# Attention with a mixture-of-experts layer on one core: loads of the opening on one queue, Wk split by two other engines, part of the next loads moved forward

## The chip, the cores and the metric

The kernel runs on one core of a Trainium2 chip. The metric is the device time in microseconds (us); less is better. The program is built with Bass and its Tile framework: inside a block called `manual_schedule` every engine runs its instructions in the order in which they are written, elsewhere a scheduler orders them, and semaphores are put in where one engine needs another's data. An engine works through its own list in order, so an instruction that waits holds up all that stand behind it.

## The reference, cut to what matters

```
# x: (2, 512, 512); 32 query heads, 8 key/value heads, head size 128
q, k, v = x @ Wq, x @ Wk, x @ Wv
probs = softmax(causal(q @ k.T / sqrt(128)))
x = layernorm(x + (probs @ v) @ Wo)
base = x @ W_base.T + b_base
w = sparsemax(x @ W_router.T + b_router)                 # 8 experts
expert = sum_e w[e] * (x @ lora_A[e]) @ lora_B[e]        # rank 16
out = layernorm(x + base + expert)
```

Everything is in 32-bit floating point. The kernel reaches that precision with several matmuls for each product: an operand is cut into a high and a low part, and high x high, high x low and low x high are added up.

## The kernel before

The work is cut into eight groups `g` (one key/value head with its four query heads), two batches `b` and four row tiles `i` of 128 queries. A unit (g, b, i) computes scores `s`, softmax weights `phl` (cut in two), their transpose `pt` (a DMA transpose issued by SP), the product `pv` with the values, and the output projection `pw`, which VectorE adds to the rows of x in the tiles `acc`. Beside the units of one group run the projections of the next: `pk`, `pq` and `pvp`, for K, Q and V.

The change lies in the first 60 us. For group 0 no scales are known yet, so the weights and x are cut in another form: `hi` is a rounded copy, `lo` is the difference (`WR` for weights, `XR` for x; the profile's tiles `wr` and `xr`). The opening is written out by hand, in one `manual_schedule` block:

- It starts with ten warm-up matmuls on zeros (`wps<-warm`, line 69).
- Loads: Wk of group 0 (tile `raw`, `load_w(4)`), the four 128-row chunks of batch 0's transposed x (`xraw`), then Wq0, Wq1, Wv, Wq2, Wq3, then batch 1's chunks of transposed x, four blocks of Wo, batch 0's transposed x again (`raw_x`), and batch 0's rows of x (`load_x(0)`, into `acc`). Chunks 0 and 2 of x are issued by ScalarE, all others by SP.
- The first projection, `PK[4]` (K of batch 0; 12 of the matmuls `park<-xr,wr`), goes chunk by chunk. For each of the four, ScalarE makes `hi` of x (`x_hi`, line 579), VectorE `lo` of x (`x_lo`, line 582), and GpSimd `hi` and `lo` of that chunk of Wk (lines 619 and 620). The other five projections follow, each of 12 matmuls, with ScalarE making `hi` and VectorE or GpSimd `lo` (lines 572 and 576).
- Maxima (`amax`, line 118, on VectorE; tile `mx`), squares (line 596) and a sum over the partitions (`total`, tile `tot`) then give the scales, by which K, Q and V leave PSUM as pairs of 16-bit tiles (lines 228 and 229).
- V is transposed by a DMA transpose (`vt`), and behind it SP issues the six blocks of W1, the weights of group 1 (tile `w1raw`), which lie in the space that `XR[0]` used (tags `base0` and `base1`).

After the block, in the scheduled part, `prepare(1, ...)` takes the maxima of the W1 blocks, finds their scales and cuts them. The rows of x of batch 1 are loaded at the first unit of batch 1 (`load_x(1)` at s == NT). These loads and `pt` are all issued by SP.

The tag `raw` has six buffers. A DMA into one waits until the last reader of what lay there is done. The tag `acc` has eight, which hold the transposed x (`xraw`) first and the rows of x later.

Of the kernel before, what the change touches and what calls it, by code (L numbers as in the profile page):

```python
# [8 lines left out]
F32 = mybir.dt.float32  # L9
# [5 lines left out]
ALU = mybir.AluOpType  # L15
AX = mybir.AxisListType

P = 128
NB, S, HID = 2, 512, 512
NT = S // P  # L20
KC = HID // P
# [15 lines left out]
def kernel(  # L37
# [18 lines left out]
    nc = tc.nc  # L56
    const = ctx.enter_context(tc.tile_pool(name="const", bufs=1))
    sb = ctx.enter_context(tc.tile_pool(name="sb", bufs=1))
# [6 lines left out]
    warm = const.tile([P, S], BF16, tag="warm", name="warm")  # L65
    nc.vector.memset(warm, 0.0)
    wps = ps.tile([P, S], F32, tag="PV", name="wps", bufs=1)
    for j in range(10):
        nc.tensor.matmul(wps, warm[:, :P], warm, start=True, stop=True)
    ident = const.tile([P, P], F32, tag="ident", name="ident")  # L70
    make_identity(nc, ident)
# [13 lines left out]
    def f(ap):  # L85
        return ap.bitcast(F32)
# [3 lines left out]
    def sync_load(dst, src):  # L90
        with tc.issue_after(hist[-3]) if len(hist) > 2 else nullcontext():
            return nc.sync.dma_start(dst, src)
# [4 lines left out]
    def load_raw(src, name, rows=False):  # L97

        raw = sb.tile([P, 512], F32, tag="rawo" if rows else "raw", name=f"raw_{name}", bufs=4 if rows else 6)
        sync_load(raw, src if len(src.shape) == 2 else src.rearrange("p a c -> p (a c)"))  # L100
        return raw
# [35 lines left out]
    def source(g, j):  # L137

        if j < 4:
            return wq[g * HPG + j]  # L140
        if j < 6:
            return (wk, wv)[j - 4][g]
        r0 = (g * HPG + j - 6) * P
        return wo[r0 : r0 + P, :]
# [43 lines left out]
    def halves(tags, name, shape):  # L188
        return [sb.tile(shape, F32R, tag=t, name=f"{name}{q}", bufs=n) for q, (t, n) in enumerate(tags)]
# [26 lines left out]
    def load_x(b):  # L216
        for t in range(b * NT, b * NT + NT):
            acc[t] = sb.tile([P, HID], F32, tag="acc", name=f"acc{t}", bufs=8)
            sync_load(acc[t], x_rows[t])

    def mm3(dst, pairs, first=True, last=True):
        n = len(pairs)
        for j, (a, b) in enumerate(pairs):
            nc.tensor.matmul(dst, a, b, start=first and j == 0, stop=last and j == n - 1)  # L224
# [9 lines left out]
    WR, XR = {}, {}  # L234

    def project(dst, g, b, j, chunks=range(KC)):
        pairs = []
        for c in chunks:
            if g:
                w2, x2 = W[(g, j)], xT[b]  # L240
                wh, wl, xh, xl = w2[:, 0, c, :], w2[:, 1, c, :], x2[:, 0, c, :], x2[:, 1, c, :]
            else:
                wh, wl, xh, xl = (a[:, c, :] for a in (*WR[j], *XR[b]))
            pairs += [(wh, xh), (wh, xl), (wl, xh)]
        mm3(dst, pairs, chunks[0] == 0, chunks[-1] == KC - 1)
# [18 lines left out]
    def pj(name, tag="pj"):  # L264
        return ps.tile([P, S], F32, tag=tag, name=name, bufs={"pj": 2, "S": 4}.get(tag, 1))
# [292 lines left out]
    JS = (4, 0, 1, 5, 2, 3)  # L558
    ROWS = (6, 7, 8, 9)
    mx = sb.tile([P, 24], F32, tag="mx0", name="mx0")  # L560
    x_raw = [[sb.tile([P, S], F32, tag="acc", name=f"xraw{b}_{c}", bufs=8) for c in range(KC)] for b in range(NB)]
    XR[0] = halves((("base0", 1), ("base1", 1)), "xr0", [P, KC, S])
    XR[1] = halves((("xr0", 1), ("xr1", 1)), "xr1", [P, KC, S])
    w_raw, PK = {}, {}
    ET = mybir.EngineType

    def load_w(j):
        w_raw[j] = load_raw(source(0, j), f"0_{j}")
        WR[j] = halves((("w", 12), ("w", 12)), f"wr{j}_", [P, KC, P])

    def w_hi(j, copy):
        copy(WR[j][0].rearrange("p a c -> p (a c)"), w_raw[j])

    def w_lo(j, engine):
        hi, lo = (a.rearrange("p a c -> p (a c)") for a in WR[j])
        engine.tensor_tensor(lo, w_raw[j], f(hi), ALU.subtract)

    def x_hi(b, c):
        nc.scalar.copy(XR[b][0][:, c, :], x_raw[b][c])

    def x_lo(b, c, engine):
        engine.tensor_tensor(XR[b][1][:, c, :], x_raw[b][c], f(XR[b][0][:, c, :]), ALU.subtract)
# [4 lines left out]
    def w_max(j):  # L587
        amax(mx[:, j : j + 1], w_raw[j])
# [7 lines left out]
        nc.scalar.activation(junk, raw, AF.Square, accum_out=dst)  # L596

    with tc.manual_schedule(engines={ET.PE, ET.DVE, ET.Activation, ET.Pool, ET.SP}):
        nc.scalar.dma_start(x_raw[0][0], xt[0, :, 0, :])
        load_w(4)  # L600
        nc.scalar.dma_start(x_raw[0][2], xt[0, :, 2, :])
        for c in (1, 3):
            nc.sync.dma_start(x_raw[0][c], xt[0, :, c, :])
        for j in JS[1:]:
            load_w(j)
        for c in range(KC):
            nc.sync.dma_start(x_raw[1][c], xt[1, :, c, :])
        wo_raw = [load_raw(source(0, j), f"0_{j}", True) for j in ROWS]
        x0_raw = [load_raw(xt[0, :, c, :], f"x0_{c}") for c in range(KC)]
        load_x(0)  # L610

        sq0 = sb.tile([P, 8], F32, tag="sq", name="sq0", bufs=2)
        sq1 = sb.tile([P, 8], F32, tag="sq", name="sq1", bufs=2)
        PK[4] = pj("park4", "pj")
        for c in range(KC):
            hi, lo = (a[:, c, :] for a in WR[4])
            raw = w_raw[4][:, c * P : (c + 1) * P]
            x_hi(0, c)
            nc.gpsimd.tensor_scalar(hi, raw, 1.0, 1.0, ALU.mult, ALU.mult)
            nc.gpsimd.tensor_tensor(lo, raw, f(hi), ALU.subtract)  # L620
            x_lo(0, c, nc.vector)
            project(PK[4], 0, 0, 4, [c])
        w_hi(0, nc.scalar.copy)
        w_lo(0, nc.vector)
        park(0, "pj")
        w_hi(1, nc.scalar.copy)
        w_lo(1, nc.gpsimd)
        park(1, "PV")
        w_hi(5, nc.scalar.copy)
        w_hi(2, nc.scalar.copy)  # L630
        w_lo(2, nc.gpsimd)
        w_hi(3, nc.scalar.copy)
        w_lo(3, nc.gpsimd)
        for c in range(KC):
            x_max(0, c)
        w_max(4)
        w_max(5)
        amax(mx[:, 6:7], mx[:, 9:13])
        for j in range(4):
            w_squares(sq0[:, j : j + 1], w_raw[j], "S")  # L640
        nc.scalar.activation(sq0[:, 4:7], mx[:, 4:7], AF.Square)
        w_lo(5, nc.vector)
        tot = total(sq0, 7, "0", "S")
        park(5, "wo")
        for c in (0, 1):
            x_hi(1, c)
            x_lo(1, c, nc.gpsimd)
        sc = sb.tile([P, 2, 8], F32, tag="sc0", name="sc0")
        SC[(0, False)] = sc
        scales(sc, tot, 7)  # L650
        x_factors(0, sc, 6)
        end_k(0, 0, PK[4])
        end_q(0, 0, 0, PK[0])
        factors(0, 0)
        end_q(0, 0, 1, PK[1])
        for c in (2, 3):
            x_hi(1, c)
            x_lo(1, c, nc.gpsimd)
        park(2, "S")
        for c in range(KC):  # L660
            x_max(1, c)
        amax(mx[:, 7:8], mx[:, 13:17])
        end_v(0, 0, PK[5])
        park(3, "S")
        for k in range(4):
            w_squares(mx[:, 17 + k : 18 + k], wo_raw[k], "S")
        amax(sq1[:, 1:2], mx[:, 17:21])
        nc.scalar.activation(sq1[:, 0:1], mx[:, 7:8], AF.Square)
        end_q(0, 0, 2, PK[2])
        tot = total(sq1, 2, "1")  # L670
        convert = split_x(0, x0_raw)
        next(convert)
        end_q(0, 0, 3, PK[3])
        sc1 = sb.tile([P, 2, 8], F32, tag="sc1", name="sc1")
        scales(sc1, tot, 2)
        SC[(0, True)] = sc1[:, :, 1:3]
        x_factors(1, sc1, 0)
        next(convert)

        w1 = [sb.tile([P, KC, S], F32, tag=f"base{q}", name=f"w1raw{q}") for q in range(2)]  # L680
        w1_raw = []
        for n, j in enumerate(JS):
            w1_raw.append(w1[n // 4][:, n % 4, :])
            sync_load(w1_raw[n].rearrange("p (c d) -> p c d", c=KC), source(1, j))

    def step_live():

# [90 lines left out]
    for s in range(len(units) - NT):  # L778
        if s < len(units):
            g, b, i = units[s]  # L780
            k = s // NT
            nx = groups[k + 1] if k + 1 < len(groups) else None
            if s == NT:
                load_x(1)
            done(unit_a(g, b, i))
            step_live()
            if nx:
                for j in ((4, 0), (1,), (5,), (2, 3))[i]:
                    proj(*nx, j)
                    advance()  # L790
            step_live()
        if s >= LB:
            done(unit_b(*units[s - LB]))
            step_live()
            advance()
        if s >= LC:
            n = s - LC
            u = units[n]
            done(unit_c(*u, n % NT == 0))
            step_live()  # L800
            if u[0] == NG - 1 and u[2] < NT - 1:
                live.append(ffn(u[2]))
        advance(True)
        if s == len(units) - 2 * NT:
            bias_row()
# [58 lines left out]
```

## Time and profile before

| | |
|---|---|
| median of 3 runs | 697.12 us (696.96 to 697.23) |
| the profiled execution | 697.11 us, of which 694.9 us are its span |
| TensorE matmul | busy 98% of the span |
| VectorE | 77% |
| ScalarE | 53% |
| GpSimd | 35% |
| DMA | 78.08 MB moved, 112 GB/s in the mean |

The span runs from the first instruction to the last. In the lines of the profile, PE is TensorE, DVE VectorE, ACT ScalarE, POOL GpSimd, SP the queue that issues most DMAs; L118 is line 118 of the kernel. A line of a timeline gives the start in us, the time it took, the engine, the line, the operation, the output and inputs with their shapes, and in brackets the idle time before it with what ended it. In the list of waits the three numbers are the total in us, how often, and the longest. Where one line joins several instructions, its time runs from the start of the first to the end of the last.

### The profile page before, as it was taken

The page shows a single profiled execution, that of the slowest core. Times are in us where ns is not written, and L with a number is a line of the kernel's source. Part 1 is how long each engine was busy: PE and PEld are TensorE (multiplying, and loading weights), DVE is VectorE, ACT ScalarE, POOL GpSimd, SP SyncE. Part 2 cuts the span into 40 slices and gives each one's busy share as a digit, 9 for nine tenths or more (in the row PEclk, how much of TensorE's full clock was granted, in tenths as well). Part 3 has the DMA queues.
Part 4 walks back from the last instruction along what each step waited for, and adds up shares of the span by engine and source line. Part 5 has one row for each costly group of instructions (what it writes and reads, how often), then busy time and mean ns, then how long its engine had stood idle before and what let it go on. Part 6 is the DMA issues. An engine that isn't in the chain of part 4 may idle for free.

```text
span 694.9 us, 10948 instructions
## 1 busy us (share of the span) xinstructions
PE 681.7 (98%) x3444; PEld 353.1 (51%) x3444; DVE 534.5 (77%) x1595; ACT 367.1 (53%) x1010; POOL 239.9 (35%) x334
## 2 busy tenths in 40 slices
PE   8999999999999999999999999999999999999996
PEld 5764545444544545454544545454544555554564
DVE  5798688778697778778697888778786785878786
ACT  5875754556365554656365554645465563446510
POOL 7665450624017150644116166146224000001022
PEclk9999999999999999999999999999999999999999
DMA  8649392637547293557448373916444261533511
GB/s 308 198 109 196 85 213 46 132 81 160 99 86 158 54 205 47 131 129 148 110 78 210 63 147 82 190 38 131 97 91 77 39 114 31 102 67 75 85 39 46
DMA packets 202026, 78.08 MB, mean 112 GB/s; under 512 B 186736, under 2 KB 186736, under 8 KB 201968
## 3 DMA queue, kind: packets, MB, share of 16 engines
q1 hardware_dynamic: 201680, 76.85, 51.1%
q8 instruction: 27, 0.44, 0.3%
q10 hardware_dynamic: 288, 0.52, 0.2%
q14 instruction: 31, 0.25, 0.1%
HBM read 29.12 MB, written 2.10 MB: 45 GB/s over the span
## 4 chain that ended last, share of the span: by engine, by line
PE 82%; DVE 8%; DMA 3%; ACT 3%; issue 2%; POOL 2%; POOLq 0%; DVEq 0%; ACTq 0%; SPq 0%
PE pw L224 20%; PE pq L224 19%; PE pv L224 13%; PE s L224 11%; PE pk L224 6%; PE pvp L224 5%; PE pa L224 4%; DVE phl L229 3%; PE park L224 2%; DVE s L342 1%; DMA raw<-in_wo_dram 1%; ACT s L347 1%; PE pb L224 1%; DMA pt<-phl 1%; ACT phl L228 1%
## 5 line engine op out<-in xcount | busy, mean ns | idle before, releaser
L347 ACT ACTIVATE s<-s,ast 128x128 f32<-128x128 f32 (+3 forms) x256 | 127.8, 499 | 165.5 <-DVE ast L342 163.7
L224 PE MATMUL pw<-w,o 128*128 128x512 f16 x768 | 176.9, 379 | 0.4 <-ACT o L228 0.2
L224 PEld LDWEIGHTS <-w 128*128 128x128 f16 x1008 | 97.8, 98 | 111.2 <-issue 0.8
L224 PE MATMUL pq<-xT,w 128*128 128x512 f16 x672 | 152.2, 379 | 0.0
L229 DVE SCALAR_TENSOR_TENSOR phl<-s,ast,phl 128x128 f16<-128x128 f32 (+3 forms) x256 | 124.6, 544 | 9.5 <-ACT phl L228 7.8
L228 ACT ACTIVATE phl<-s,ast 128x128 f16<-128x128 f32 (+3 forms) x256 | 116.7, 539 | 28.6 <-DVE ast L322 16.2
L342 DVE CUSTOM_DVE_ANT_0 s<-s,mask,lm 128x128 f32<-128x128 f32 (+3 forms) x256 | 126.6, 553 | 1.4 <-PE s L224 1.3
L224 PEld LDWEIGHTS <-o 128*128 128x128 f16 x768 | 74.7, 98 | 90.3 <-DVE o L229 0.8
L224 PE MATMUL s<-k,q 128*128 128x128 f16 (+3 forms) x768 | 117.7, 299 | 2.7 <-DVE phl L229 2.3
L224 PE MATMUL pv<-pt,vt 128*128 128x512 f16 x480 | 114.4, 379 | 1.6 <-DMA pt<-phl 1.6
L224 PEld LDWEIGHTS <-q 128*128 128x128 f16 x768 | 68.3, 98 | 50.6 <-issue 4.9
L256 POOL TENSOR_SCALAR lm<-sc,xs 128x1 f32<-128x1 f32 x15 | 4.0, 264 | 226.2 <-DVE sc L132 139.6
L115 POOL TENSOR_TENSOR w<-raw,w 128x512 f16<-128x512 f32 x68 | 77.2, 1155 | 0.3
L224 PEld LDWEIGHTS <-vt 128*128 128x128 f16 x480 | 46.7, 100 | 55.2 <-DMA pt<-phl 2.4
L396 DVE SCALAR_TENSOR_TENSOR acc<-pw,lm,acc 128x512 f32<-128x512 f32 x64 | 47.9, 748 | 33.0 <-PE pw L224 33.0
L229 DVE SCALAR_TENSOR_TENSOR o<-pv,o 128x512 f16<-128x512 f32 x64 | 43.9, 685 | 30.7 <-ACT o L228 30.5
L112 POOL TENSOR_SCALAR raw<-raw,sc 128x512 f32<-128x512 f32 x68 | 46.3, 692 | 57.6 <-DVE sc L133 57.6
L228 ACT ACTIVATE o<-pv 128x512 f16<-128x512 f32 x64 | 39.6, 618 | 34.3 <-PE pv L224 34.2
L118 DVE TENSOR_REDUCE mx<-raw 128x1 f32<-128x512 f32 x66 | 42.8, 678 | 14.7 <-DMA raw<-in_wo_dram 14.6
L347 ACT ACTIVATION_READ_ACCUMULATOR s<-s,ast 128x1 f32 x256 | 51.5, 201 | 0.0
L229 DVE SCALAR_TENSOR_TENSOR q<-pq,q 128x512 f16<-128x512 f32 x56 | 38.3, 688 | 15.1 <-ACT q L228 14.9
L228 ACT ACTIVATE q<-pq 128x512 f16<-128x512 f32 x56 | 34.0, 612 | 26.0 <-PE pq L224 25.8
(141 smaller groups left out, 612.1 us busy)
## 6 DMA issues: line engine op xcount, KB each, us to landing
raw<-in_wo_dram SPq DMA_DIRECT2D x32, 256.0 KB, 3.6
raw<-in_wq_dram SPq DMA_DIRECT2D x28, 256.0 KB, 4.5
raw_x<-in_xt_dram SPq DMA_DIRECT2D x8, 256.0 KB, 4.7
acc<-in_x_dram SPq DMA_DIRECT2D x8, 256.0 KB, 4.8
pt<-phl SPq DMA_TRANSPOSE x128, 3.8
out_dram<-y SPq DMA_DIRECT2D x8, 256.0 KB, 2.0
raw<-in_wk_dram SPq DMA_DIRECT2D x7, 256.0 KB, 3.6
raw<-in_wv_dram SPq DMA_DIRECT2D x7, 256.0 KB, 4.6
```

The costliest lines, as they stand in the source:

```text
L112: nc.gpsimd.tensor_scalar(view, view, by, 1.0, ALU.mult, ALU.mult)
L115: return first.ins, nc.gpsimd.tensor_tensor(lo, view, hi, ALU.subtract).ins
L118: nc.vector.tensor_reduce(dst, view, AX.X, ALU.max, apply_absolute_value=True)
L224: nc.tensor.matmul(dst, a, b, start=first and j == 0, stop=last and j == n - 1)
L228: nc.scalar.activation(hi, psrc, AF.Copy, scale=by)
L229: return nc.vector.scalar_tensor_tensor(lo, psrc, by, hi, ALU.mult, ALU.subtract).ins
L256: engine.tensor_scalar(lm[:, 4:5], sc[:, 0, 4:5], XS[b][0], 1.0, ALU.mult, ALU.mult)
L342: nc.vector.tensor_tensor_reduce(out=sc[:, :n], in0=sc[:, :n], in1=mask[:, S - n :], scale=lm[:, h : h + 1], scalar=BIG, op0=ALU.add, op1= ...
L347: nc.scalar.activation(sc[:, :n], sc[:, :n], AF.Exp, bias=st[:, 0, h : h + 1], scale=-1.0, accum_out=st[:, 1, h : h + 1])
L396: nc.vector.scalar_tensor_tensor(a, pw, LM[(g, b)][:, 7:8], a, ALU.mult, ALU.add)
```

## The change

The warm-up has nine matmuls. All first loads are issued by SP: x chunk 0, Wk, x chunks 1 to 3, then the weights as before. Wk is cut by ScalarE (`hi`) and VectorE (`lo`) in two pieces, chunk 0 and chunks 1 to 3, in place of GpSimd's eight instructions. W1's Wk and Wq0 are loaded into the tag `raw` behind `raw_x` and ahead of batch 0's rows of x; the other four blocks of W1 stay behind `vt`, all in the tag `base0`. Batch 1's rows of x are loaded directly behind those four, at the end of the block.

```diff
-    for j in range(10):
+    for j in range(9):
         nc.tensor.matmul(wps, warm[:, :P], warm, start=True, stop=True)
...
-        nc.scalar.dma_start(x_raw[0][0], xt[0, :, 0, :])
-        load_w(4)
-        nc.scalar.dma_start(x_raw[0][2], xt[0, :, 2, :])
-        for c in (1, 3):
+        for c in range(KC):
             nc.sync.dma_start(x_raw[0][c], xt[0, :, c, :])
+            if c == 0:
+                load_w(4)
...
         x0_raw = [load_raw(xt[0, :, c, :], f"x0_{c}") for c in range(KC)]
+        w1_raw = [load_raw(source(1, j), f"1_{j}") for j in JS[:2]]
         load_x(0)
...
         for c in range(KC):
-            hi, lo = (a[:, c, :] for a in WR[4])
-            raw = w_raw[4][:, c * P : (c + 1) * P]
             x_hi(0, c)
-            nc.gpsimd.tensor_scalar(hi, raw, 1.0, 1.0, ALU.mult, ALU.mult)
-            nc.gpsimd.tensor_tensor(lo, raw, f(hi), ALU.subtract)
             x_lo(0, c, nc.vector)
+            if c < 2:
+                n = slice(0, 1) if c == 0 else slice(1, KC)
+                hi, lo = (a[:, n, :].rearrange("p c d -> p (c d)") for a in WR[4])
+                raw = w_raw[4][:, n.start * P : n.stop * P]
+                nc.scalar.copy(hi, raw)
+                nc.vector.tensor_tensor(lo, raw, f(hi), ALU.subtract)
             project(PK[4], 0, 0, 4, [c])
...
-        w1 = [sb.tile([P, KC, S], F32, tag=f"base{q}", name=f"w1raw{q}") for q in range(2)]
-        w1_raw = []
-        for n, j in enumerate(JS):
-            w1_raw.append(w1[n // 4][:, n % 4, :])
-            sync_load(w1_raw[n].rearrange("p (c d) -> p c d", c=KC), source(1, j))
+        w1 = sb.tile([P, KC, S], F32, tag="base0", name="w1raw")
+        for n, j in enumerate(JS[2:]):
+            w1_raw.append(w1[:, n, :])
+            sync_load(w1[:, n, :].rearrange("p (c d) -> p c d", c=KC), source(1, j))
+        load_x(1)
...
-            if s == NT:
-                load_x(1)
             done(unit_a(g, b, i))
```

In the order that the scheduler gives, the maxima of W1's Wk and Wq0 now stand earlier in VectorE's list: the first ahead of the low part of V, the second between two score tiles of unit (0,0,0). On TensorE `pv` of unit (0,0,0) comes ahead of all `pvp` matmuls instead of behind six of them, and `s` of unit (0,0,3) follows `pw` of unit (0,0,0) with no `pq` matmuls between.

## The prediction

> **What bounds the kernel now.** I read the page first, then TensorE's waits, then the chain of waits for the first 60 us, then single engines' timelines where the chain changes hands.
>
> ```profile
> PE 681.7 (98%) x3444; PEld 353.1 (51%) x3444; DVE 534.5 (77%) x1595; ACT 367.1 (53%) x1010; POOL 239.9 (35%) x334
> ```
>
> TensorE is busy for 98% of the 694.9 us span, so a gap in it that closes early comes off the end: after the first 60 us its own waits add up to 2.0 us. Its waits of the first 75 us, in the list of waits (total, times, longest):
>
> ```profile
> PE pv L224 <- DMA pt<-phl: 1.3, 1, 1.3
> PE s L224 <- DVE phl L229: 1.2, 1, 1.2
> PE park L224 <- POOL wr L619: 0.4, 2, 0.2
> ```
>
> Three places. First the start, in the chain of waits (start us, us, what), where GpSimd's split of Wk paces the first projection:
>
> ```profile
> 0.72 4.23 DMA raw<-in_wk_dram
> ...
> 9.02 0.71 POOL wr L619
> ...
> 9.81 0.78 POOL wr L620
> ...
> 10.64 5.98 PE park L224 x25
> ```
>
> From 10.64 on TensorE has no gap for 20 us. Second, VectorE stands at the maximum of W1's Wk block, which has only then landed, with the softmax steps of unit (0,0,0) queued behind it (VectorE's timeline, then TensorE's):
>
> ```profile
> 29.95 0.69 DVE L118 TENSOR_REDUCE mx<-w1raw 128x1 f32<-128x512 f32 x1 [1.66 <-DMA w1raw<-in_wk_dram]
> ...
> 31.64 0.68 DVE L118 TENSOR_REDUCE mx<-w1raw 128x1 f32<-128x512 f32 x1
> 32.40 0.61 DVE L229 SCALAR_TENSOR_TENSOR phl<-s,ast,phl 128x128 f16<-128x128 f32 x2
> ```
> ```profile
> 32.81 0.82 PE L224 MATMUL s<-k,q 128*128 128x256 f16 x6 [1.16 <-DVE phl L229]
> 33.88 2.57 PE L224 MATMUL pq<-xr,wr 128*128 128x512 f32 x10 [0.25 <-DVE ast L322]
> ```
>
> Third, batch 1's rows of x stand in SP's queue ahead of the transposes of unit (0,0,2), and TensorE waits for those (SP's timeline; the chain; TensorE's timeline):
>
> ```profile
> 47.27 1.50 SPq L92 DMA_DIRECT2D acc<-in_x_dram  x3
> 48.95 4.44 SPq L95 DMA_TRANSPOSE pt<-phl  x2
> ```
> ```profile
> 50.66 5.86 DMA pt<-phl
> ```
> ```profile
> 56.56 2.12 PE L224 MATMUL pv<-pt,vt 128*128 128x512 f16 x9 [1.35 <-DMA pt<-phl]
> ```
>
> The change touches all three.
>
> **Part 1: the start.** Eight GpSimd instructions go (L619 x4 at 0.63, L620 x4 at 0.66 us mean: 5.1 us of the queue that paces the chain). ScalarE gains two copies of Wk, VectorE two subtractions, each 128x128 and 128x384. No row shows them in fp32r; nearest are 128x128 and 128x384 `phl`, 0.38 and 0.59 us on ScalarE, 0.35 and 0.61 on VectorE. Bounds: nothing, if all fits into waits (VectorE waits 5.4 us in all for `xr` here), and 0.9 us on each engine. I count them whole, as both engines now carry the chain.
>
> Loads: SP issues all five first ones at about 0.42 us each, so by 2.9; a load passes in 0.65 us (the semaphore events put Wq0, Wq1, Wv and Wq2 at 8.86, 9.51, 10.20 and 10.85). Now Wk lands at 4.95, x chunk 0 at 5.12, chunks 1 to 3 at 6.10, 6.60, 8.21. On one queue Wk still has one load ahead: 5.0. Chunk 0, first, lies between 3.6 and 5.1; I take 4.3. Chunks 1, 2: 5.65, 6.3; chunk 3 between 7.0 and 8.2.
> - ScalarE: x0 hi 4.3 to 4.95, Wk hi chunk 0 to 5.4, x1 hi 5.67 to 6.3, rest of Wk hi to 6.85, x2 hi to 7.5, x3 hi to 8.4 at worst.
> - VectorE (0.70 for an x lo): x0 lo to 5.7, Wk lo chunk 0 to 6.0, x1 lo 6.3 to 7.0, rest of Wk lo to 7.6, x2 lo to 8.3, x3 lo 8.4 to 9.1.
> - TensorE: chunk 0 from 5.4 at 0.43 us each, chunk 1's last at 7.6, chunk 2's three by 8.8, chunk 3's last issued about 9.4.
>
> Now it is issued at 10.64: 1.2 us. Wq0, landing at up to 8.86, has its low part by about 10.2 and takes some of that: I carry **1.1 us**, between 0.3 (all first data 0.8 later) and 1.6. Of ScalarE's sums of squares and VectorE's maxima, which end at 14.56 and 13.9 now, nothing moves later than TensorE needs for `tot` (15.3): slack 0.6 us. If it went, `tot` would wait for that much. GpSimd, freed, has Wq1's low part at 11.4; it is read at 12.9.
>
> The tenth warm-up matmul (0.43 us, ending 5.4) goes; it would have stood in the way of a start at 5.4. That costs nothing unless the clock suffers. The rows: warm-ups 0.43 us apart, parks from 11.2 on 0.23 apart; the fast spacing is there from about 7 us. [...] By the row, TensorE stood still for 0.5 us at 5.4 and was granted the clock all the same; here the gap is 5.0 to 5.4, and the first term stays 1.1. [...]
>
> **Part 2: two blocks of W1 sooner.** Their loads go ahead of batch 0's four rows of x: these land 1.3 us later (2 x 0.65), at under 24 us, and are first read at 49.8: free. W1's Wk and Wq0 land near 21, before VectorE reads them. But both maxima (0.6 us of VectorE's time each) now stand earlier. The first is ahead of V's low part, which releases the transpose `vt` and behind it W1's other four loads. So `vt` is issued at 24.67 - 1.1 + 0.6 = 24.17. It lands 4.2 us after issue, and the first and second loads behind it are there 1.0 and 2.45 us later (28.91, 29.93, 31.37 now): 29.4 and 30.9. VectorE reaches the third maximum at 29.0 and waits 0.4, ends it at 30.0, and waits for the fourth to 30.9. It does `phl` from 31.5 (32.40 now), K's low part to 32.75 (33.82). **The wait is not removed, it passes to the next two blocks**: TensorE, ready at 30.4, waits to 31.8 for `s` and to 32.8 for `pq`, against 33.88. The lead stays 1.1 us and doesn't grow: 0 from this part. Bound above: without the wait VectorE itself sets 32.1, 0.7 us more. Below: a landing 1 us later takes 1 us.
>
> **Part 3: batch 1's rows sooner.** SP issues four loads more ahead of `pt` of unit (0,0,0). [...] W1's loads now end at 34.17 and `pt`, issued at 33.04, lands at 35.45. With two loads more in all and the lead, the ring is empty near 34.9 and both `pt` have landed at 36.6. TensorE (now 38.8, with six `pvp` ahead that come after it in the new order, 1.4 us) is there at 36.2: a new wait of 0.4. By the row alone (2.5 us from issue at 33.9 to landing), 36.4 and 0.2. I take 0.4. By unit (0,0,1) VectorE and DMA have lead again, and about 0.3 comes back at the S buffers, which are free when TensorE comes to them. So the lead is 1.0 near 47 us. There `s` of unit (0,0,3) follows `pw` with no `pq` between, so its cover of 1.6 us is gone: `phl` is written at 46.0 and 46.5, TensorE needs it at 46.1 and 46.75: just in time.
>
> In return SP issues the transposes of unit (0,0,2) when `phl` is written, about 46.5 and 49.0, with no load in front: landed near 53, and TensorE comes at 55.2 - 1.0 = 54.2. The 1.35 us go whole. What is late next is the softmax of the same unit, within 0.5 us.
>
> **Sum**, against the profiled execution's own 697.11 us (span 694.9; median 697.12): 1.1 + 0 - 0.4 + 0.3 + 1.35 = 2.35, so 694.8. What follows runs with no gap, so nothing gives it back.
>
> **The rivals.**
> - Partly taken back (25%): first data later, a missed clock window, lost cover before `s` of (0,0,3), or pt later by a microsecond. Each takes 0.3 to 1; for it, VectorE and SP are tighter than before; against, none was a bound but by these loads. About 1.2 in all: 696.0.
> - W1's blocks are in time (20%). The window of DMA from 25 to 29 us shows one instruction fetch (q8) and a hole in `vt`'s transfer from 26.8 to 28. Without the collision, `vt` lands 1.5 us sooner and VectorE sets the pace: 0.7 + 0.3 more, 693.8. Against: fetch and `vt` both hang on VectorE's chain and move together.
> - Slower (6%): `pt` of unit (0,0,0) is stuck behind batch 1's rows. The transposes of unit (0,0,2) took 6.2 us from issue to landing behind three such loads. If `pt` takes that from 33.9, it lands at 40.1, 3.5 us after my 36.6, and the gain of 2.35 turns into a loss of 1.1; another collision of 1.5 makes it 699.6 at worst, 698.6 in the middle. It decides from a landing at about 39.
> - The change does nothing (4%): the waits move elsewhere in full, 697.1.
>
> **How the numbers follow.** Likeliest (45%): 694.8, by itself 694.0 to 695.6. 0.2% is 1.4 us, about what a measurement of this kernel can tell from no change; faster than that means under 695.7. All of the likeliest and of the second rival lie there, and a fifth of the first: 0.45 + 0.20 + 0.05 = 0.70. Same: the rest of the first, and the last: 0.24. Slower: 0.06. The range, 693.0 to 696.7, leaves out the slow case, the last, and the ends of the others.
>
> **What would show it.** Right: the last matmul of the first 12 parks starts between 9.2 and 10.3; `mx<-w1raw` still waits for its load near 29 to 31, under 1.7 us; `pv` at 54 does not wait for `pt`; `pv` near 36 does, by under 1 us. Wrong: the first 12 end later than 10.6 or run 0.43 us apart beyond 7 us; `pv` near 36 waits over 2 us; or a lead of 2 us at 60 us that is not there at the end.

## The result and the profile after

| | before | after |
|---|---|---|
| median | 697.72 us (696.96 to 698.78, 6 runs) | 694.33 us (693.16 to 695.05, 6 runs) |
| the profiled execution | 697.11 us, span 694.9 | 694.67 us, span 692.9 |

The ratio of the times is 0.9949, with a 95% interval of 0.9935 to 0.9962: 3.6 us less, between 2.7 and 4.5. The two profiled executions are 2.44 us apart, 2.06 of it inside the span (VectorE's last `y` starts at 689.14 us, 691.20 before); the other 0.4 lies outside it and has no row. The executions of one and the same kernel differ by the clock that TensorE was granted: of 129 of the kernel before, taken beside the experiments, 65 had a mean clock of 0.997 or more, as the two profiled ones have, and a median of 696.9 us, the others 698.6 us.

The page's first line is hardly changed, but for GpSimd's eight instructions that are gone:

```profile
PE 681.1 (98%) x3443; PEld 353.5 (51%) x3443; DVE 534.0 (77%) x1597; ACT 367.9 (53%) x1012; POOL 235.0 (34%) x326
```

TensorE's waits of the first 75 us (total, times, longest):

```profile
...
PE s L224 <- DVE phl L229: 0.8, 1, 0.8
PE park L224 <- ACT wr L622: 0.7, 2, 0.5
PE tot L123 <- ACT q L228: 0.3, 1, 0.3
PE pq L224 <- DVE k L229: 0.2, 1, 0.2
```

The wait of `pv` for `pt`, 1.3 us before, is not in the list any more. That of `s` for `phl` is smaller but still there. The start waits for ScalarE's part of Wk where it waited for GpSimd's. TensorE's timeline has the numbers (start, us, what; in brackets the idle time ahead and what ended it):

```profile
7.35 8.26 PE L224 MATMUL park<-xr,wr 128*128 128x512 f32 x33 [0.48 <-ACT wr L622]
15.45 0.28 PE L123 MATMUL tot<-sq,ones 128*128 128x7 f32 x2
...
31.96 0.81 PE L224 MATMUL s<-k,q 128*128 128x256 f16 x6 [0.83 <-DVE phl L229]
32.94 1.20 PE L224 MATMUL pq<-xr,wr 128*128 128x512 f32 x4 [0.17 <-DVE k L229]
...
36.63 0.81 PE L224 MATMUL pv<-pt,vt 128*128 128x512 f16 x3
...
54.22 2.12 PE L224 MATMUL pv<-pt,vt 128*128 128x512 f16 x9
```

Set against the kernel before, `tot` stood at 16.46 us there and stands at 15.45: a lead of 1.01. `s` came from 32.81 to 31.96 (0.85), `pq` from 33.88 to 32.94 (0.94), and `pv` of unit (0,0,2) from 56.56 to 54.22 (2.34). At the end of the span 2.06 are left.

VectorE's timeline shows why TensorE gained nothing more near 31 us. It now waits for the third block of W1 (Wq) where it waited for the first (Wk):

```profile
30.01 0.69 DVE L118 TENSOR_REDUCE mx<-w1raw 128x1 f32<-128x512 f32 x1 [0.75 <-DMA w1raw<-in_wq_dram]
...
31.56 0.61 DVE L229 SCALAR_TENSOR_TENSOR phl<-s,ast,phl 128x128 f16<-128x128 f32 x2
```

And SP's timeline has batch 1's rows (`acc`) directly behind W1's blocks and out of the way of the later transposes:

```profile
28.72 1.80 SPq L92 DMA_DIRECT2D acc<-in_x_dram  x4
...
46.34 12.74 SPq L95 DMA_TRANSPOSE pt<-phl  x4
```

### The profile page after: what moved, and what is told of

The parts are those of the page before. It is cut to its first block, busy times and chain, and to the rows that moved or that the text cites. A ratio compares the mean times of both kernels' runs of the same rounds, so it can differ in the third digit from the quotient of the medians.

```text
span 692.9 us, 10942 instructions
## 1 busy us (share of the span) xinstructions
PE 681.1 (98%) x3443; PEld 353.5 (51%) x3443; DVE 534.0 (77%) x1597; ACT 367.9 (53%) x1012; POOL 235.0 (34%) x326
## 4 chain that ended last, share of the span: by engine, by line
PE 82%; DVE 9%; ACT 3%; DMA 2%; issue 2%; POOL 1%; SPq 0%; POOLq 0%; DVEq 0%; ACTq 0%
PE pw L224 21%; PE pq L224 20%; PE pv L224 13%; PE s L224 12%; PE pk L224 5%; PE pvp L224 5%; PE pa L224 4%; DVE phl L229 3%; DVE s L342 1%; DMA raw<-in_wo_dram 1%; PE park L224 1%; ACT s L347 1%; DVE mx L118 1%; PE pb L224 1%; ACT phl L228 1%
## 5 line engine op out<-in xcount | busy, mean ns | idle before, releaser
L115 POOL TENSOR_TENSOR w<-raw,w 128x512 f16<-128x512 f32 x70 | 79.6, 1156 | 0.3
L118 DVE TENSOR_REDUCE mx<-raw 128x1 f32<-128x512 f32 x68 | 44.3, 678 | 15.8 <-DMA raw<-in_wo_dram 15.7
L228 ACT ACTIVATE q<-pq 128x512 f16<-128x512 f32 x56 | 34.0, 613 | 24.5 <-PE pq L224 24.3
```

The costliest lines, as they stand in the source:

```text
L115: return first.ins, nc.gpsimd.tensor_tensor(lo, view, hi, ALU.subtract).ins
L118: nc.vector.tensor_reduce(dst, view, AX.X, ALU.max, apply_absolute_value=True)
L228: nc.scalar.activation(hi, psrc, AF.Copy, scale=by)
```

## The experiments

The difference in us is worked out from the ratio and the median of the kernel before in the same group of runs (697.72 us for the change; 698.06 for runs 1 to 4, 697.5 for 5 to 8, 697.43 for 9 to 11, 698.02 for 12); the last column is the interval of the ratio in us.

| kernel | median us | ratio | difference us | interval |
|---|---|---|---|---|
| the change | 694.33 | 0.9949 | -3.6 | -4.5 to -2.7 |
| 1 start alone | 695.04 | 0.9958 | -2.9 | -4.0 to -2.0 |
| 2 two W1 blocks alone | 700.96 | 1.0039 | +2.7 | +1.7 to +3.6 |
| 3 batch 1's rows alone | 696.32 | 0.9978 | -1.5 | -2.2 to -0.8 |
| 4 change, four W1 blocks early | 693.27 | 0.9935 | -4.5 | -5.7 to -3.4 |
| 5 change without the rows | 696.4 | 0.9981 | -1.3 | -2.1 to -0.6 |
| 6 change without W1's blocks | 695.2 | 0.9961 | -2.7 | -3.7 to -1.7 |
| 7 change without the start | 701.56 | 1.0045 | +3.1 | +2.0 to +4.3 |
| 8 change, six W1 blocks early | 695.09 | 0.9952 | -3.3 | -4.7 to -2.0 |
| 9 before, stall filled | 698.04 | 1.0008 | +0.6 | -0.3 to +1.3 |
| 10 change, ten warm-ups | 694.51 | 0.9957 | -3.0 | -3.8 to -2.2 |
| 11 loads of the start alone | 696.53 | 0.9990 | -0.7 | -1.3 to -0.1 |
| 12 split of Wk alone | 697.1 | 0.9989 | -0.8 | -1.7 to +0.2 |

**1. The start alone**: nine warm-ups, first loads on SP, Wk split by ScalarE and VectorE.

```diff
-    for j in range(10):
+    for j in range(9):
...
+        for c in range(KC):
+            nc.sync.dma_start(x_raw[0][c], xt[0, :, c, :])
+            if c == 0:
+                load_w(4)
...
+                nc.scalar.copy(hi, raw)
+                nc.vector.tensor_tensor(lo, raw, f(hi), ALU.subtract)
```

> The kernel before with the new start alone (nine warm-ups, first loads on SP, Wk split by ScalarE and VectorE). My theory: the start is worth 1.1 us, everything in VectorE's chain up to the transpose vt moves with it, and with vt the loads of W1 behind it; so VectorE's wait for W1's Wk stays about 1.7 us long and is only passed earlier, and the wait of pv of unit (0,0,2) for pt stays at 1.3. Time 1.1 us under before. Rival: W1's landing is set by the DMA queue and not by vt, so the lead is eaten in that wait (it grows to 2.7 us) and the time is that of before.

It took 695.04 us. TensorE's waits of the first 75 us:

```profile
PE s L224 <- DVE phl L229: 1.7, 1, 1.7
...
PE pv L224 <- DMA pt<-phl: 0.7, 1, 0.7
```

In this execution TensorE's timeline lists no idle time between 5.3 and 15 us, and `tot` came at 14.94, 1.5 us sooner than before. But 0.5 us more of waiting for `phl` (1.7 against 1.2) took that much back: W1's loads stand behind `vt` in SP's list (issued from 26.12 and at 24.67 us in the kernel before), and the first of them was there only 0.87 us sooner (VectorE's maximum of it starts at 29.08 us, 29.95 before). One thing was not expected: `pv` of unit (0,0,2) waited only 0.65 us for `pt`, against 1.35, though batch 1's rows stood in SP's queue where they had stood before. In time the start is the largest part.

**2. W1's two blocks alone.**

```diff
+        w1_raw = [load_raw(source(1, j), f"1_{j}") for j in JS[:2]]
         load_x(0)
...
+        for n, j in enumerate(JS[2:]):
```

> The kernel before with two blocks of W1 loaded ahead of batch 0's rows of x alone. My theory: VectorE still waits, for the third block, by 0.4 to 1.1 us, and has spent 0.6 us more ahead of vt; the time is within 0.4 us of before. Rival, which is what the edit looks like: the wait of 1.66 us and TensorE's 1.16 us behind it go, and the time is 1.2 to 1.4 us under before.

It is slower than before, which neither theory had. VectorE's timeline tells why: with the old start the scheduler put the maximum of W1's Wk into VectorE's list directly behind `tot`, ahead of the scales, on which everything that cuts K and Q of batch 0 waits:

```profile
20.57 0.69 DVE L118 TENSOR_REDUCE mx<-raw 128x1 f32<-128x512 f32 x1 [3.57 <-DMA raw<-in_wk_dram]
21.18 0.16 DVE L132 TENSOR_SCALAR sc<-tot 128x7 f32<-128x7 f32 x1
```

VectorE stood for 3.57 us, and TensorE for 2.67 us ahead of its first `s`, at 27.75 us. (The list names ScalarE's squares, line 596, as what ended this wait; they stand behind K and Q in ScalarE's list, which start at 22.41 and 23.00 us, when the scales are there, and run from 25.75 us on.) So this run measures the place of the maxima, not the loads.

**3. Batch 1's rows alone.**

```diff
+        load_x(1)
...
-            if s == NT:
-                load_x(1)
```

> The kernel before with batch 1's rows of x loaded at the end of the opening block alone. My theory: pv of unit (0,0,2) no longer waits 1.35 us for pt, pt of unit (0,0,0) lands later but TensorE comes to it at 38.8 us only and doesn't wait; time 1.35 us under before. Rival: pt of unit (0,0,0) stands behind ten loads, TensorE waits 1 us or more near 39 us, and the time is that of before.

1.5 us less, which fits the 1.35 us of `pv`'s wait. Its trace shows less: `pv` of unit (0,0,2) still waited 0.43 us for `pt`, so that 0.9 of the 1.35 us were gone, and its profiled execution waited longer for `phl` than any other (2.0 us). TensorE's timeline:

```profile
57.72 2.12 PE L224 MATMUL pv<-pt,vt 128*128 128x512 f16 x9 [0.43 <-DMA pt<-phl]
```

**4. Four of W1's blocks early**, two more than in the change, in the space of `y`.

```diff
         w1_raw = [load_raw(source(1, j), f"1_{j}") for j in JS[:2]]
+        for j in JS[2:4]:
+            w1_raw.append(sb.tile([P, HID], F32, tag="y", name=f"w1y{j}", bufs=2))
+            sync_load(w1_raw[-1].rearrange("p (c d) -> p c d", c=KC), source(1, j))
```

> The changed kernel with four blocks of W1 loaded ahead of batch 0's rows of x instead of two (W1's Wq1 and Wv into the two buffers of tag y, which nothing else uses before the end). The scheduler reorders some instructions near 30 us. Theory that VectorE's wait for w1raw at 30 us (0.75 us in the changed kernel) costs TensorE time: it goes, and the time is 0.7 us under the changed kernel, the lead at 33 us is 1.6 to 1.8 us against 0.94. Rival: VectorE's own work sets the pace there, the lead stays under 1.2 us and the time is that of the changed kernel within 0.3 us.

693.27 us, the lowest of all. TensorE's waits of the first 75 us show the wait of `s` for `phl` gone, and what is late next, K's low part:

```profile
PE pq L224 <- DVE k L229: 0.6, 1, 0.6
PE pv L224 <- DMA pt<-phl: 0.3, 1, 0.3
```

The span is 690.7 us, 2.1 under the change's. `pk` began at 24.07 us, 0.8 sooner than in the change, and this lies ahead of the waits that the two blocks were to shorten; the waits near 31 us were shorter by 0.4, and `pv` of unit (0,0,1) gave 0.3 back. At `pv` of unit (0,0,2) it was 0.8 us ahead (53.42 against 54.22). The rest came later: `pk` of the next group began 1.55 us sooner (136.69 against 138.24). So most of the 2.1 us in this pair of traces is not the two blocks' wait. The interval overlaps the change's: that four blocks are better than two is likely, not certain.

**5. The change without batch 1's rows** (`load_x(1)` back at `s == NT`).

```diff
-        load_x(1)
...
+            if s == NT:
+                load_x(1)
```

> The changed kernel with batch 1's rows of x loaded at the first unit of batch 1 again (start and W1's two blocks kept). Theory: the transposes of unit (0,0,2) stand behind these loads again and TensorE waits 1 to 1.4 us for pt near 55 us; its time is about 1.4 us over the changed kernel's, 695.7 us, with a lead over the kernel before near 1.0 us up to 54 us and none gained there. Rival, that batch 1's rows were behind idle queues anyway and the gain came with the start: 694.3 us, no wait for pt near 55 us.

2.2 us slower than the change by the two ratios (0.0032). TensorE's timeline has the wait again, and SP's the rows between the transposes:

```profile
54.60 2.12 PE L224 MATMUL pv<-pt,vt 128*128 128x512 f16 x9 [0.82 <-DMA pt<-phl]
```
```profile
45.80 1.72 SPq L95 DMA_TRANSPOSE pt<-phl  x1
47.57 1.42 SPq L92 DMA_DIRECT2D acc<-in_x_dram  x2
49.08 9.46 SPq L95 DMA_TRANSPOSE pt<-phl  x3
```

In the traces the two are closer: `pv` waits 0.82 us more here, and the profiled executions are 0.55 us apart. Together with run 3, where the rows alone took 1.5 us off, this shows that the rows' place in SP's queue costs time. It does not show that all of the 1.35 us is the rows' (runs 1, 3 and 6).

**6. The change without W1's two blocks** (all six behind `vt`).

```diff
-        w1_raw = [load_raw(source(1, j), f"1_{j}") for j in JS[:2]]
...
+        for n, j in enumerate(JS):
```

> The changed kernel with all six blocks of W1 loaded behind vt again (start and batch 1's rows kept). Theory of the prediction, that the two blocks only pass VectorE's wait on to the next two: the same as the changed kernel, 694.3 us within 0.4. Rival, that they do shorten the wait: with the earlier start alone TensorE waited 1.7 us for phl near 30 us, so s of unit (0,0,0) waits 1.5 to 2 us here instead of 0.8 and the time is 695.1 to 695.6 us, and some runs have a lower mean clock than the changed kernel's.

0.8 us slower than the change by the ratios, with intervals that overlap. In the profiled execution `s` waited 1.20 us for `phl` against 0.83. And `pv` of unit (0,0,2) waited for `pt`, although batch 1's rows are out of the way here (TensorE's timeline, then SP's):

```profile
55.34 2.12 PE L224 MATMUL pv<-pt,vt 128*128 128x512 f16 x9 [0.49 <-DMA pt<-phl]
```
```profile
48.56 12.24 SPq L95 DMA_TRANSPOSE pt<-phl  x4
```

SP issued that transpose at 48.56 us, against 46.34 in the change. Without the two blocks VectorE's list has the old order, in which all four `phl` of this unit come together from 47.35 us on; in the change two come at 45.12 us and two at 47.49. So the blocks bring an order with them, and the last 0.5 us of `pv`'s wait goes with it: with rows and blocks both moved (the change, runs 4, 7, 8 and 10) no trace has that wait, with the rows moved and the old order both have (0.43 in run 3). All in all they are worth between nothing and some 2 us in time, and 0.4 and 0.5 us at these two waits in the trace.

**7. The change without the start.** The edit is run 1's, backwards.

```diff
-    for j in range(9):
+    for j in range(10):
...
+            nc.gpsimd.tensor_scalar(hi, raw, 1.0, 1.0, ALU.mult, ALU.mult)
+            nc.gpsimd.tensor_tensor(lo, raw, f(hi), ALU.subtract)
```

> The changed kernel with the old start (ten warm-ups, loads on two queues, GpSimd's split of Wk); W1's two blocks and batch 1's rows kept. Here the list order puts the maximum of W1's Wk directly behind VectorE's part of the scales, as in the kernel with the two blocks alone. Theory that the parts add up: 1.1 us over the changed kernel, 695.4 us. Rival, that the maximum's place in VectorE's list decides: VectorE stands 3 to 4 us at it near 20 us, TensorE waits over 2 us near 27 us and goes to half clock, and the time is 697.5 to 700 us.

The rival held in its mechanism, and the time, 701.56 us, lies above even its range. VectorE's timeline has the same place for the maximum as in run 2:

```profile
20.61 0.69 DVE L118 TENSOR_REDUCE mx<-raw 128x1 f32<-128x512 f32 x1 [3.47 <-DMA raw<-in_wk_dram]
```

The parts of this change don't add up, since one of them moves instructions that another one's loads feed. In the changed kernel the maxima stand behind those of batch 1's x, at 23.05 and 25.62 us, and don't wait.

**8. All six of W1's blocks early.**

```diff
+        for j, tag, w in zip(JS[4:], ("xf", "ffnbias"), (HID, HID + NE)):
+            w1_raw.append(sb.tile([P, w], F32, tag=tag, name=f"w1t{j}")[:, :HID])
```

> The changed kernel with all six blocks of W1 loaded ahead of batch 0's rows of x, none behind vt. Theory: with four blocks early (693.27 us) TensorE's wait for phl near 31 us is gone already, and what is left there is a wait of 0.6 us for K's low part; six take at most that: 692.7 to 693.3 us. Rival, that six loads more push batch 0's rows or the maxima into the way of vt: 693.8 us or more, with a wait for acc or phl on TensorE before 60 us.

The waits near 31 us are gone altogether in the trace (span 691.7 us), but `tot` waited 0.7 us at 24.5 us for ScalarE, and the time is 695.09 us, with a wide interval. That is the time of the rival, without the wait that it named. Four of its seven executions had a mean clock under 0.997. No run shows more to be had from W1's loads than four blocks give.

**9. Before, with the stall at 31.6 us filled.**

```diff
+            if s == 1:
+                fill = ps.tile([P, S], F32, tag="PV", name="fill", bufs=1)
+                with tc.issue_after(last_q):
+                    for j in range(6):
+                        nc.tensor.matmul(fill, warm[:, :P], warm, start=True, stop=True)
             done(unit_a(g, b, i))
```

> The kernel before with six matmuls on zeros (1.3 us of TensorE) put between the twelve pq and the s that waits for phl near 31.6 us; they compute nothing that is used. Nothing else is moved. Theory: TensorE's clock falls to half for a window of 3.4 us after a stretch in which it stood for more than about half of a window (it did in the traces with 2.0, 2.6 and 2.7 us of wait, not in those with up to 1.7 us), and executions with a mean clock under 0.997 are in good part such ones. Then filling the stall costs 0.1 to 0.3 us in the others, and the share of executions under 0.997 falls from a half to under a quarter: median 696.9 to 697.3 us against 697.5 to 698 of before. Rival, that the low clock has nothing to do with that stall (it is set at the start, or is there throughout): the share stays at a half and the median is 0 to 0.3 us above before's.

The theory fell: 7 of 14 executions still had a mean clock under 0.997, and the time is 0.6 us above before's, with an interval that includes no change at all. The edit was not clean, though. The scheduler moved two maxima ahead of the second pair of `phl`, and TensorE still waited for `phl` in two pieces, 0.58 us at 33.3 and 0.86 us at 35.96 us. The trace of this run has its half-clock window elsewhere, at the other end of the kernel. TensorE's timeline, then busy time and granted clock by stretch (the column behind POOL is the clock):

```profile
645.47 1.01 PE L224 MATMUL s<-k,q 128*128 128x256 f16 x6 [1.10 <-DVE phl L229]
```
```profile
core 0: us, PE busy (x) PEld busy (x) DVE busy (x) ACT busy (x) POOL busy (x), PEclk, DMA share, GB/s
644.40:647.90 3.50, 2.40 (x12) 1.47 (x12) 3.11 (x10) 2.19 (x7) 0.00 (x0) 0.99 0.83 155
647.90:651.30 3.40, 3.40 (x10) 2.66 (x9) 2.24 (x9) 2.30 (x10) 0.00 (x0) 0.50 0.41 79
```

A wait of 1.10 us like this one is in the traces of before (ahead of 643.84 us) and of the change (ahead of 642.07) too, and cost no window there: the granted clock is 1.00 from 642 to 660 us in both. In this trace a window followed, and so it did in run 10's (0.51 from 645.3 to 648.8 us) and run 7's (0.50 from 649.67 to 653.08 us).

**10. The change with ten warm-ups.**

```diff
-    for j in range(9):
+    for j in range(10):
```

> The changed kernel with ten warm-up matmuls again. By the row (the tenth is in the way of a start at 5.4 us and the clock needs it not): 0 to 0.3 us over the changed kernel, 694.3 to 694.6 us. [...]

694.51 us, the same as the change within its interval; in the trace the first `park` starts at 5.46 us instead of 5.41. The tenth is neither needed nor in the way. As a near twin of the change it also shows how much luck a profiled execution has: here `pv` at 37.29 us waited 0.69 us for `pt`, which in the change's own trace had landed 0.13 us before TensorE came.

**11. The loads of the start alone.**

```diff
-        nc.scalar.dma_start(x_raw[0][0], xt[0, :, 0, :])
-        load_w(4)
-        nc.scalar.dma_start(x_raw[0][2], xt[0, :, 2, :])
-        for c in (1, 3):
+        for c in range(KC):
             nc.sync.dma_start(x_raw[0][c], xt[0, :, c, :])
+            if c == 0:
+                load_w(4)
```

> The kernel before with only the loads of the start put on one queue (x chunk 0, Wk, x chunks 1 to 3); ten warm-ups and GpSimd's split of Wk kept. Theory: GpSimd's eight instructions pace the first projection from Wk's landing at 5.0 us, which doesn't move: nothing gained, as before within 0.3 us, the last matmul of the first twelve issued at 10.5 to 10.7 us. Rival, that the landing of x chunk 3 at 8.2 us paces it: up to 0.7 us faster.

0.7 us less, yet not at the start: GpSimd's last step (line 620 before, 619 here) is at 10.11 us, 9.81 before, and `tot` stands at 16.47 us against 16.46. GpSimd's timeline:

```profile
10.11 0.46 POOL L619 TENSOR_TENSOR wr<-raw,wr 128x128 fp32r<-128x128 f32 x1
```

The theory held for the start; where the 0.7 us come from is open; 16 of 22 executions had a mean clock of 0.997 or more, against half of before's.

**12. The split of Wk alone.**

```diff
-            nc.gpsimd.tensor_scalar(hi, raw, 1.0, 1.0, ALU.mult, ALU.mult)
-            nc.gpsimd.tensor_tensor(lo, raw, f(hi), ALU.subtract)
...
+                nc.scalar.copy(hi, raw)
+                nc.vector.tensor_tensor(lo, raw, f(hi), ALU.subtract)
```

> The kernel before with only the split of Wk given to ScalarE (high part) and VectorE (low part); loads on two queues and ten warm-ups as before. Theory: the gain at the start is the split's, up to what x chunk 3's landing at 8.2 us leaves: its high part at 8.9, low part at 9.6, the last matmul of the first twelve issued at 9.7 against 10.6 us, 0.8 us of lead; with the old place of the loads behind vt a gain of 0.7 to 1.5 us, 696.0 to 696.8 us. Rival, that loads and split help only together (chunk 3 late, Wk's pieces in front of x chunks 1 and 2): the last of the twelve at 10.3 us or later and the time within 0.4 us of before's.

0.8 us less, with an interval that includes no change at all. Its trace cannot decide, because in it TensorE stayed at the slow spacing to 10.5 us. Busy time and number of matmuls from 7.0 to 10.5 us, here and then in run 1:

```profile
7.00:10.50 3.50, 3.50 (x8) 2.28 (x8) 3.15 (x6) 3.42 (x7) 0.57 (x1) 1.00 1.04 399
```
```profile
7.00:10.50 3.50, 3.50 (x14) 2.23 (x14) 3.15 (x6) 2.72 (x6) 0.72 (x1) 1.00 1.01 387
```

Both are busy throughout, with 8 matmuls in one (0.44 us each) and 14 in the other (0.25 us each). `tot` came at 16.69 us, nothing gained. The clock column shows 1.00 in both; but in the trace's own clock record the full clock begins at 10.59 us here and at 6.93 us in run 1, and nothing is recorded ahead of that, so this slow start is to be read from the spacing. Ahead of it TensorE had stood from 5.62 to 6.11 us. Loads and split each give 0.7 to 0.8 us alone and 2.9 us together. In run 11 the chain was left on GpSimd, which was not moved; that here it was left on the landing of x is argued, not shown. The intervals are wide enough that the two could also just add up.

## Why the prediction was right, point by point

The sum was 2.35 us. The two profiled executions are 2.44 apart, the medians 3.4, and the interval begins at 2.7: the gain in time is larger than the sum by 0.3 us at least. Two things that the sum left out account for much of it.

The first is the clock. Of the kernels with the new start (the change, runs 1, 4 to 6, 8 and 10) 20 of 73 executions had a mean clock under 0.997, of the kernel before 64 of 129; at 1.7 us each, the estimate of the last section, that is some 0.4 us on average. The share differs from kernel to kernel (none of 6 in run 1, 4 of 7 in run 8), so this is rough, and why the new start should make such executions rarer is open. The second lies outside the span: 2.06 to 2.20 us in every one of the 129 executions before, 1.75 to 1.81 in all six of the change. That is 0.35 us which no step had, and why is open too.

Without both, the sum comes out well: over executions with a mean clock of 0.997 or more the median span is 694.8 us before (65 executions) and 692.3 for the change (5), 2.5 us less. The same comparison gives 1.65 for the start alone (run 1), 1.3 for the rows alone (run 3), 1.05 without the rows (run 5) and 2.1 without W1's blocks (run 6).

- **Start, 1.1 us.** Measured 1.01 at `tot` in the change's trace, which is the least of all with the new start: `tot` came between 14.94 and 15.45 us in the seven of them; with the old start it came between 15.96 and 16.65 (before and runs 2, 3, 7 and 9). The instructions cost what was counted: on ScalarE 0.30 and 0.51 us, on VectorE 0.28 and 0.55. One landing was off: x chunk 1 came at 6.24 us, not 5.65, and the last of the first twelve matmuls was issued at 9.77, not 9.4 (10.64 before). In time the start alone took 2.9 us off, more than its trace accounts for: there `s` is only 1.0 us ahead of before's (31.82 against 32.81), and the last `y` 1.2 (689.98 against 691.20). All six of its executions had a mean clock of 0.997 or more, which is one part of the difference.
- **Warm-ups.** The row held: nine or ten make no difference (694.33 and 694.51 us, run 10). In the traces' clock records the full clock begins at 6.53 us in the kernel before, with ten, and at 6.51 in the change and 6.93 in run 1, with nine. Neither of the traces with nine shows the missed clock window of the first rival. A late full clock has its price all the same: run 12's trace, with ten, pays about 0.2 us on some six matmuls (0.44 us each against 0.25).
- **Two blocks of W1, 0 us.** Held near 31 us, with the mechanism: the wait passes to the next blocks. `vt` was issued at 24.47 us (24.17 predicted; `ck`, line 198, took 0.69 us on VectorE against 0.35, so that much lead was gone ahead of it). VectorE waited 0.75 us for the third block (0.4 predicted) and not for the fourth, `phl` began at 31.56 (31.5), `s` at 31.96 (31.8), `pq` at 32.94 (32.8). Run 4 suggests that the wait that stayed cost time. What the step did not count is that the order which comes with the blocks helps `pt` of unit (0,0,2) (run 6, 0.5 us); that gain stands in the sum under the rows.
- **Rows of x of batch 1.** The new wait of `pv` near 36 us, predicted as 0.4 and named as a sign of being right, was absent in the changed kernel's trace and 0.69 in its twin's. (In the change batch 1's rows had landed by 35.45 us and the two `pt` behind them at 36.07 and 36.5, in the order of issue; 36.6 was predicted. That `pt` lands behind the loads issued ahead of it was the author's estimate from one row of before: issued at 33.04 us, landed at 35.45, with W1's last block landed at 34.17.) Of the 0.3 that was to come back after it nothing can be seen either: the lead was 0.94 at `pq` and 0.99, without the 1.35, at `pv` of unit (0,0,2). That the two terms nearly cancel is luck. `s` of unit (0,0,3) came at 46.09 us (46.1 predicted), and `pv` of unit (0,0,2) at 54.22 (54.2) without a wait. Runs 3 and 5 put 1.5 and 2.2 us on this part. But the 1.35 us is not the rows' alone: the wait was 0.65 with the new start only (run 1), 0.82 with start and blocks (run 5), 0.43 and 0.49 with the rows moved and the old order (runs 3 and 6), and nothing with all three parts.
- **"What follows runs with no gap, so nothing gives it back"** is the step that did not hold, by 0.3 us: TensorE's lead was 2.34 us from 54 to 81 us, 2.07 at 82 us and 2.06 at the end. TensorE's timeline, first after, then before:

```profile
81.88 1.46 PE L224 MATMUL pv<-pt,vt 128*128 128x512 f16 x6
```
```profile
83.95 1.46 PE L224 MATMUL pv<-pt,vt 128*128 128x512 f16 x6
```

  This `pv` needs a `pt` which SP issued only 1.79 us sooner than before (77.31 against 79.10) and which landed at 81.74 us, 0.1 us after TensorE was ready. The way back leads to batch 1's `raw_x`: SP issues these loads at 67.57 us, no sooner than before (67.49). ScalarE's timeline shows its conversions waiting for them, with the exponentials of the next unit queued behind:

```profile
70.79 0.72 ACT L111 ACTIVATE xT<-raw_x,sc 128x512 f16<-128x512 f32 x1 [2.51 <-DMA raw_x<-in_xt_dram]
72.11 2.03 ACT L111 ACTIVATE xT<-raw_x,sc 128x512 f16<-128x512 f32 x3 [0.60 <-DMA raw_x<-in_xt_dram]
74.05 0.43 ACT L347 ACTIVATE s<-s,ast 128x256 f32<-128x256 f32 x1
```

  In the kernel before these exponentials began at 75.82 us and waited for VectorE. In run 5 SP issued the same loads at 66.51 us, and its lead of 1.96 us at 61 us was still 1.9 at the end. That this chain takes the lead back is read from the traces; a kernel with those loads earlier was not tried. Nor is the stretch behind 82 us free of gaps: the change's lead was 1.90 at 138 us, 1.79 at 216 us and 2.06 at the end, and in run 11 a lead of 0.39 at 61 us grew to 1.20. So the span of a single pair of traces is good to about a microsecond, and that the profiled pair's 2.44 came so near the sum, with 0.3 lost here and 0.4 gained outside the span, is luck.
- **The rivals.** The slower one needed `pt` of unit (0,0,0) to land after 39 us: it landed at 36.5. "W1 in time" did not happen here; with four blocks early (run 4) the wait for `phl` was gone. Runs 2 and 7 show a slower case that the prediction had not thought of, a maximum placed too early in VectorE's list, at 2.7 and 3.1 us. The changed kernel's own order does not have it.

## What to carry to other kernels

When a load is moved forward, look where its consumer now stands in its engine's list: a scheduler may move that up too, and the engine then waits for the load with everything queued behind it, VectorE for 3.57 us in run 2. When one wait on a path is shortened, ask which load or engine ends next, here the third block of W1 and later `raw_x`. Edits at one hand-over (loads and split) may pay together, so that measuring each alone undersells them; here the intervals leave it likely, not certain. A single profiled execution shows the mechanism, but not sizes under a microsecond.

## What the runs showed of the hardware

**Half clock followed waits of 2.0 to 2.7 us, and two of 1.1.** In the traces' clock records, up to TensorE's last matmul, half clock comes in stretches of 3.41 us (run 7's last from 649.67 to 653.08 us), one or two together; such a stretch is called a window here. In run 2 TensorE was busy for 1.08 of 3.4 us and was then held at half clock for two windows; in run 3 it was busy for 1.40 of 3.4 us, and one window followed. Run 2's busy time and granted clock by stretch, then run 3's:

```profile
24.00:27.40 3.40, 1.08 (x5) 0.66 (x4) 3.37 (x10) 3.40 (x9) 2.50 (x2) 1.00 0.00 0
27.40:30.80 3.40, 2.39 (x11) 1.80 (x11) 3.05 (x10) 3.17 (x9) 0.69 (x1) 0.50 0.10 22
30.80:34.20 3.40, 3.40 (x11) 2.42 (x10) 1.48 (x8) 2.69 (x9) 3.32 (x4) 0.50 1.12 203
```
```profile
30.80:34.20 3.40, 1.40 (x9) 0.95 (x8) 3.00 (x14) 1.92 (x6) 2.85 (x5) 0.98 0.99 355
34.20:37.60 3.40, 3.40 (x10) 2.34 (x9) 3.27 (x10) 3.40 (x9) 2.90 (x4) 0.52 0.98 291
```

In the second window of run 2 TensorE is busy all the time with 11 matmuls; in the next 3.4 us, at full clock, it did 18. The waits ahead of a window were 2.67 us in run 2, 2.0 in run 3 and 2.6 in run 7, and near 645 us 1.10 us in runs 9 and 10. Waits near 31 us cost no window in the traces of before (1.16 us) and of runs 1, 5, 6 and 12 (1.7, 1.12, 1.20 and 1.8 us), whose mean clocks are 0.997 or 0.998. What exactly is counted is not settled, and busy time alone does not separate these cases. In the 3.4 us around the 1.10 us, the kernel before was busy for 2.27 (642.51 to 645.91 us), and full clock followed; run 10 was busy for 2.26 (641.9 to 645.3 us), and half clock followed.

A window in which TensorE is busy throughout, at a granted clock of 0.50, is put at 1.7 us (an estimate, half of the 3.41 measured). That is also what separates the medians of the kernel before, 696.9 and 698.6 us, and one such window is what the traces with a mean clock of 0.996 show (runs 3, 9 and 10). So a mean clock under 0.997 most likely means one window or more at half clock. By the same estimate the stall of 2.0 us in run 3 cost 1.7 us more and that of 2.67 us in run 2, by its 2.39 and 3.40 us of busy time at half clock, some 2.9, and run 2's 2.7 us over before are partly that.
